# Two edits in the written order of a graph-attention and expert kernel: where layer 1 normalises its softmax, and where the plan of a layer's remainder stands

## The chip, the cores and the metric

The kernel runs on one core of a Trainium2 chip. A core has five engines that matter here: TensorE (PE) for matmuls and transposes, VectorE (DVE), ScalarE (ACT), GpSimd (POOL) and SyncE (SP), which issues most DMAs. They run side by side and wait for each other through semaphores. The metric is the device time of one execution in microseconds, as the median of several runs.

## The reference

Two layers, each of a graph attention over 128 graphs of 64 nodes and a mixture of eight experts, on 8192 rows of 256 numbers in float32:

```
x = x + elu( softmax(mask(e)) @ (LN(x) @ W) )      e[i,j] = (Wh a1)[i] + (Wh a2)[j]
                                                   layer 1: e = leaky_relu(e)
z = LN(x)
layer 0:  x = x + z + sum over the 2 best experts of w_e * (gelu(z W1_e + b1_e) W2_e + b2_e)
layer 1:  x = x +     sum over the 2 best experts of w_e * (relu(z W1_e + b1_e) W2_e + b2_e)
```

The hidden width of an expert is 256 in layer 0 and 512 in layer 1. The two weights of a row come from a softmax over its two best router scores.

## The kernel before

**Blocks.** The 8192 rows of a layer are 16 blocks of 512 rows (four tiles of 128 rows). Both layers make 32 blocks in a row. For each block a Python generator `attend` emits the attention and another, `route`, emits normalisation, router and the writing of each row into the lists of its two experts in DRAM. A `yield` ends a stage; a call `a(i)` or `r(i)` emits the next stage of block i.

**Slots.** Expert work comes in slots of 256 rows of one expert. The expert of a slot is known only on the chip: `plan` (L560 to 602) works out with small DVE instructions, every time a block has been routed, which expert lists can fill the next four slots, and writes the numbers into a table; SP reads the table into registers and fetches rows (`fetch`, L682) and weights (L733 to L741). What is left in the lists at the end is handled by `fill_up` and `rests` (L516 to 529 and L603 to 668): SP appends eight pieces of padding to the lists, DVE works out a table for 12 more slots, some of which hold two halves. That happens after block 8 and block 15 of layer 0 and after block 15 of layer 1. In this text it is "the plan of the rest".

A slot is worked in three parts: `x` (transposes px, L764, copied by DVE to xT, L768), `h` (matmuls L846, activation by ACT, L855) and `y` (matmuls L877 into py, then an addition on DVE, L884, that empties py). py has one PSUM buffer. In layer 0 the result rows go to two rows of a buffer in DRAM per token; the attention of layer 1 first adds these to its input with the weights of the router: eight DVE instructions a block, L267, "the sum of result rows". In layer 1 the weighted rows are added to the output by a DMA (L922).

**The order.** The order of instructions on PE, DVE, ACT and SP is exactly that of emission; only POOL's is left to the scheduler. The main loop (from L1038) has one step per block: t counts from 3, n = t+1. In one step the kernel finishes the attention of block n, routes block t, starts the attention of block t+2, and works four slots (five where many are waiting: `more`). The stages of `attend` that matter are, in order: the sum of result rows (L263 to 274), statistics, normalised rows, transposes, the product with W (L290), its diagonal (L301), scores and exp (L309 to L328, ending on ACT), the **normalise** (a reciprocal L334 and a product L335 on DVE), the transposes of the attention (pp, L339, and copies L341, L342), the product po (L348), and the ELU. Around the edits the loop before is:

```
        r(t)                      # router matmuls, first of the two best
        if t + 2 != NB:
            a(t + 2)              # the sum of result rows
        y()
        a(n)                      # normalise
        (h if more else x)()
        r(t)
        a(n)                      # transposes of the attention
        y()
```

Near the start of the step stands `r(t - 1)`, the last stage of the routing of the block before: `plan`, and where due `fill_up` and `rests`.

## Time and profile before

| what | us |
|---|---|
| median of 3 runs (lowest, highest) | 1437.01 (1436.83, 1442.47) |
| the profiled execution, and its span | 1675.06, 1673.3 |
| PE busy in the span | 1305.4 |
| DVE busy | 875.1 |
| POOL busy | 743.9 |
| ACT busy | 647.5 |
| mean granted clock of PE | 0.882 |

The profiled execution takes 238 us more than the runs. A line of the timeline has the start, the busy time, the engine, the line of the kernel, the operation and what it writes and reads, how many instructions are merged in it, and in brackets the idle time of that engine before it with what ended it. A line of the list of waits has the waiting instruction, the one that released it, and then the microseconds in total, how often, and the longest.

### The profile page before, as it was taken

To read this page: it belongs to the slowest core of one execution; us is meant where nothing else is said; L and a number is where in the kernel's file an instruction comes from. 1 tells how busy PE (TensorE), PEld (TensorE's weight loads), DVE (VectorE), ACT (ScalarE), POOL (GpSimd) and SP (SyncE) were. 2 spreads that over 40 slices of the span, in tenths; PEclk is the share of its full clock that TensorE was granted. 3 is DMA by queue.
4 is the path that set the end of the run, shared out by engine and by line. 5 is a ranking of instruction groups with operands and counts; after the bars stand their busy time and mean duration, and the time that the engine had idled before them with its cause. 6 is when DMAs were issued, how large, how long until landed. Compare 5 with 4: busy or idle time off the path is not lost. (4 is left out here: it accounts for less than half of the span.)

```text
span 1673.3 us, 22326 instructions
## 1 busy us (share of the span) xinstructions
PE 1305.4 (78%) x6240; PEld 1100.9 (66%) x6240; DVE 875.1 (52%) x3390; ACT 647.5 (39%) x1550; POOL 743.9 (44%) x729
## 2 busy tenths in 40 slices
PE   7657777777777667766768888988888988869994
PEld 5546665655665556555657777877777777658883
DVE  4555755574455566745565555655555654442331
ACT  5534444444433434333333434333344434223331
POOL 3164444444445543334442455444455444544324
PEclk9668988998888898788789999988889888989997
DMA  6535555575565654656765768666777656677873
GB/s 194 143 124 176 197 167 168 167 219 167 167 184 189 228 186 152 204 171 198 219 219 156 218 194 234 197 169 193 208 215 213 172 134 185 169 218 223 238 211 65
DMA packets 262829, 311.69 MB, mean 186 GB/s; under 512 B 40615, under 2 KB 219950, under 8 KB 262704
## 3 DMA queue, kind: packets, MB, share of 16 engines
q1 hardware_dynamic: 219552, 225.02, 43.7%
q0 software_dynamic: 43152, 85.24, 19.1%
q8 instruction: 50, 0.82, 0.2%
q14 instruction: 75, 0.61, 0.1%
HBM read 212.25 MB, written 99.75 MB: 186 GB/s over the span
## 5 line engine op out<-in xcount | busy, mean ns | idle before, releaser
L846 PE MATMUL ph_s<-xT_s,wc_s 128*128 128x256 f32 (+1 forms) x1760 | 402.1, 380 | 57.3 <-DVE xT_s L768 22.8
L877 PE MATMUL py_s<-wc_s,hT_s 128*128 128x256 f32 x1648 | 425.6, 411 | 21.8 <-issue 14.0
L846 PEld LDWEIGHTS ph_s<-xT_s,wc_s 128*128 128x128 f32 x1760 | 327.0, 198 | 116.3 <-DVE xT_s L768 29.9
L877 PEld LDWEIGHTS py_s<-wc_s,hT_s 128*128 128x128 f32 x1648 | 331.7, 207 | 75.9 <-issue 16.6
L922 POOL DMA_INDIRECT out_dram<-ys_s,to_s x135 | 212.8, 1576 | 366.7 <-ACT ys_s L919 215.7
L499 POOL DMA_INDIRECT lists<-tn_r,ix_r x256 | 249.5, 975 | 102.9 <-issue 71.9
L855 ACT ACTIVATE hT_s<-ph_s,wc_s 128x256 f32<-128x256 f32 (+1 forms) x440 | 175.8, 457 | 278.5 <-issue 117.2
L290 PE MATMUL pw_g<-gw,xt_g 128*128 128x258 f32 x512 | 157.6, 459 | 134.0 <-ACT wh_g L297 74.0
L893 POOL DMA_INDIRECT res<-ys_s,to_s x142 | 146.2, 1029 | 259.7 <-DVE erc_g L334 177.9
L290 PEld LDWEIGHTS pw_g<-gw,xt_g 128*128 128x128 f32 x512 | 109.5, 228 | 169.5 <-ACT wh_g L297 83.3
L768 DVE COPY xT_s<-px_s 128x512 f32<-128x512 f32 (+1 forms) x140 | 95.5, 682 | 204.4 <-remote 89.4
L884 DVE TENSOR_TENSOR ys_s<-py_s,wc_s 128x512 f32<-128x512 f32 (+1 forms) x149 | 97.4, 654 | 188.6 <-PE py_s L877 180.7
L419 PE MATMUL pl_r<-rw,xt_r 128*128 128x8 f32 x512 | 81.8, 295 | 45.4 <-DVE xt_r L255 40.9
L419 PEld LDWEIGHTS pl_r<-rw,xt_r 128*128 128x128 f32 x512 | 82.1, 246 | 51.7 <-DVE xt_r L255 45.2
L297 ACT COPY wh_g<-pw_g 128x258 f32<-128x258 f32 x128 | 47.0, 375 | 162.4 <-remote 82.0
L919 ACT ACTIVATE ys_s<-ys_s,cf_s 128x256 f32<-128x256 f32 x135 | 61.4, 500 | 105.7 <-DVE ys_s L884 105.4
L240 ACT ACTIVATE tn_r<-xb_g,nb_r,rs_r 128x256 f32<-128x256 f32 x128 | 66.5, 590 | 86.3 <-DVE nb_r L238 55.5
L240 ACT ACTIVATE xn_g<-xs,nb_g,rs_g 128x256 f32<-128x256 f32 x128 | 66.4, 590 | 66.3 <-DVE nb_g L238 66.3
L764 PE MATMUL px_s<-ident,xg_s 128*128 128x128 f32 x554 | 85.7, 278 | 0.2 <-DMA xg_s<-lists 0.2
L764 PEld LDWEIGHTS px_s<-ident,xg_s 128*128 128x128 f32 x554 | 70.7, 146 | 13.0 <-issue 1.0
L348 PE MATMUL po_g<-wh_g,pT_bd 128*128 128x256 f32 x256 | 70.8, 425 | 8.5 <-ACT pT_bd L342 7.0
L342 ACT COPY pT_bd<-pp_g 64x256 f32<-64x256 f32 x32 | 11.7, 365 | 163.7 <-DVE pT_bd L341 160.6
(503 smaller groups left out, 1583.8 us busy)
## 6 DMA issues: line engine op xcount, KB each, us to landing
wc_s<-in_w_dram SPq DMA_DIRECT2D x142, 512.0 KB
wc_s<-in_w_dram SPq DMA_DIRECT2D x156, 256.0 KB
xg_s<-lists SPq DMA_DIRECT2D x64, 260.0 KB
xg_s<-lists SPq DMA_DIRECT2D x64, 258.0 KB
yb<-res SPq DMA_DIRECT2D x16, 1024.0 KB
wc_s<-bcat SPq DMA_DIRECT2D x78, 129.0 KB
wc_s<-bcat SPq DMA_DIRECT2D x71, 130.0 KB
xs<-in_x_dram SPq DMA_DIRECT2D x16, 512.0 KB
```

The lines of the kernel that those rows point to most:

```text
L240: nc.scalar.activation(outs(t), xb[:, t, :], AF.Identity, bias=nb[:, t : t + 1], scale=rs[:, t : t + 1])
L290: nc.tensor.matmul(pw, lhsT=xt[:, k, t * P : (t + 1) * P], rhs=gw[l][:, k, :], start=(k == 0), stop=(k == KD - 1),)
L419: nc.tensor.matmul(pl[:, t, :], lhsT=tT[:, k, t * P : (t + 1) * P], rhs=rw[l][:, k, :], start=(k == 0), stop=(k == KD - 1),)
L499: ins = nc.gpsimd.indirect_dma_start(out=lists[l], out_offset=bass.IndirectOffsetOnAxis(ap=ix[:, k, t : t + 1], axis=0), in_=tn[:, t, 0 : ...
L764: nc.tensor.transpose(px[:, c, t * P : (t + 1) * P], xg[:, t, c * P : (c + 1) * P], ident)
L768: nc.vector.tensor_copy(xT[:, :, 0 : st * P], px[:, :, 0 : st * P])
L846: nc.tensor.matmul(ph[:, j, r], lhsT=w[:, o : o + P], rhs=xT[:, c, r], start=(c == 0), stop=(c == KD - 1),)
L855: nc.scalar.activation(hT[:, f + j, r], ph[:, j, r], AF.Gelu if l == 0 else AF.Relu, bias=w[:, OB1[l] + f + j : OB1[l] + f + j + 1],)
L877: nc.tensor.matmul(py[:, t, :], lhsT=hT[:, f, t * P : (t + 1) * P], rhs=w[:, O2[l] + f * D : O2[l] + (f + 1) * D], start=(f == 0), stop=(f ...
L884: nc.vector.tensor_tensor(ys[:, r, :], py[:, r, :], w[:, OB2[l] : OB1[l]].unsqueeze(1).to_broadcast([P, r.stop - r.start, D]), ALU.add,)
L893: ins = nc.gpsimd.indirect_dma_start(out=res[sl["part"]], out_offset=self.row(sl, t), in_=ys[:, t, :], in_offset=None, bounds_check=2 * N - 1,
L922: ins = nc.gpsimd.indirect_dma_start(out=out, out_offset=self.row(sl, t), in_=ys[:, t, :], in_offset=None, compute_op=ALU.add,)
```

## The change

Two things change, both in the order of emission; no instruction is added or taken away. First, the stage with the sum of result rows is cut into two stages of four instructions each. In a step whose block n belongs to layer 1 (t = 15 to 30) the order on DVE becomes: first half of the sum, normalise, second half of the sum, then `y`. In layer 0 the sum does not exist and the normalise stays behind `y`. Second, the last stage of `route` is cut in two, so that `fill_up` and `rests` come later: no longer behind `plan` near the start of the step, but in a new call `r(t - 1)` near its end, between the third or fourth `y` and the last routing stages of block t. The counts of the other calls are adapted so that every other stage stands where it stood.

```diff
-        if l > 0:
-            for t in range(TT):
+        for i in range(2):
+            for t in range(TT * l * i // 2, TT * l * (i + 1) // 2):
                 for k in range(2):
                     nc.vector.scalar_tensor_tensor(
...
-        yield
+            yield
         stats = ln_stats(xs, name)
...
         if b - (CUT if b >= CUT and l == 0 else 0) >= LAG:
             slots.take(l, b, SB, plan(l, f"p{l}_{b}", SB))
+        yield
         if b == NB - 1 or (l == 0 and b == CUT - 1):
             fill_up(l, b)
             slots.take(l, b, SF, rests(l, f"p{l}_{b}r"), True)
...
         r(t)
+        early = n < len(blks) and blks[n]["l"] == 1
+        if t + 2 != NB:
+            a(t + 2)
+        if early:
+            a(n)
         if t + 2 != NB:
             a(t + 2)
         y()
-        a(n)
+        if not early:
+            a(n)
         (h if more else x)()
         r(t)
         a(n)
         y()
-        a(t + 2, 1 + (t + 2 == NB))
+        a(t + 2, 1 + 2 * (t + 2 == NB))
...
         y()
         a(t + 2)
+        r(t - 1)
         r(t)
         r(t)
         y()
...
-    r(len(blks) - 1)
+    r(len(blks) - 1, 2)
     slots.fetch()
```

More of the change, by code (lines that the diff above doesn't have):

```diff
@@ L995, in adj_ffn_kernel @@
     load(FIRST)
-    a(0, 2)
+    a(0, 3)
     make_gw(0)
     a(0)
-    a(1, 2)
+    a(1, 3)
     token2 = counted("token2", [P, NT], [[2 * P, NT]], 0, 2)
@@ L1002, in adj_ffn_kernel @@
     place = counted("place", [P, ST], [[P, ST]], 0, 1)
-    att = lambda b: [(a, b)] * 9 + [(a, b, 2), (a, b)]
+    att = lambda b: [(a, b, 2)] + [(a, b)] * 8 + [(a, b, 2), (a, b)]
     chains = [
@@ L1008, in adj_ffn_kernel @@
         (8, att(3) + [(r, 3)] * 2),
-        (12, [(a, 4)] * 3),
+        (12, [(a, 4, 2), (a, 4), (a, 4)]),
     ]
@@ L1035, in adj_ffn_kernel @@
         turn += 1
-    r(2)
+    r(2, 2)
     slots.fetch()
```

## The prediction, made before the changed kernel was run

> **What bounds the kernel now.** I read the page first, then the list of waits, then the stretch of the timeline around the normalise of the softmax in several steps, and then the places where the plan of the rest stands and is to stand.

> ```profile
> PE 1305.4 (78%) x6240; PEld 1100.9 (66%) x6240; DVE 875.1 (52%) x3390; ACT 647.5 (39%) x1550; POOL 743.9 (44%) x729
> ...
> PE pp_g L339 <- DVE ee_g L335: 25.2, 19, 4.3
> ...
> PE pp_g L339 <- DVE l_r L445: 18.3, 5, 7.6
> ```

> TensorE (PE) is the busiest engine, so what counts is time in which PE waits. The transposes of the attention (pp, L339) wait for VectorE (DVE). 7.1 us of the first wait line lie in layer 0, and so does one wait of 7.6 in the second (its releaser was last to report; the normalise stands just ahead of it). Layer 1, which alone is changed, has 18.1 + 10.7 = **28.9 us in 16 steps**. Two such places, the second in a late step (t = 22), the first at t = 15:

> ```profile
> 641.06 3.75 DVE L267 SCALAR_TENSOR_TENSOR xs<-yb,cs,xs 128x256 f32<-128x256 f32 x8
> 641.46 0.60 PE L764 MATMUL px_s<-ident,xg_s 128*128 128x128 f32 x4
> 644.72 0.69 DVE L884 TENSOR_TENSOR ys_s<-py_s,wc_s 128x512 f32<-128x512 f32 x1
> 645.53 0.43 DVE L335 TENSOR_TENSOR ee_g<-ee_g,erc_g 128x256 f32<-128x256 f32 x1
> 646.10 1.04 PE L339 MATMUL pp_g<-ident,ee_g 128*64 128x128 f32 x4 [4.04 <-DVE ee_g L335]
> 646.93 3.62 PE L877 MATMUL py_s<-wc_s,hT_s 128*128 128x256 f32 x8
> ...
> 1046.91 3.75 DVE L267 SCALAR_TENSOR_TENSOR xs<-yb,cs,xs 128x256 f32<-128x256 f32 x8
> 1051.80 0.60 PE L764 MATMUL px_s<-ident,xg_s 128*128 128x128 f32 x4
> 1052.00 0.69 DVE L884 TENSOR_TENSOR ys_s<-py_s,wc_s 128x512 f32<-128x512 f32 x1 [1.35 <-PE py_s L877]
> 1052.82 0.42 DVE L335 TENSOR_TENSOR ee_g<-ee_g,erc_g 128x256 f32<-128x256 f32 x1
> 1053.38 0.60 PE L339 MATMUL pp_g<-ident,ee_g 128*64 128x128 f32 x4 [0.98 <-DVE ee_g L335]
> ```

> See the order on DVE: eight rows of the sum (L267), the addition that empties py (L884, "y-add"), the normalise (L335); then PE may go on. At 641 DVE itself is late: PE stood for 4.04 us behind a sum that the normalise does not need. At 1052 it is PE that comes late to y-add, since its matmuls ran at half clock; the wait is 0.98. The last line at 641 also shows the price of a long wait: eight matmuls at 3.62 us, where the y of the step at 743.07 takes 1.89 for eight.

> **The profiled execution and the runs.** It took 1675.06 us (span 1673.3), the median of the runs is 1437.01: 238 us less. The waits that end on "remote" (DVE xT_s 89.4, ACT wh_g 82.0, DVE xt_r 70.4, ACT hT_s 34.4) and the half-clock stretches behind them are my candidates for that difference. So I price each part twice: as the profile has it, and with PE at full clock and no such wait. The second is the one I take for the runs.

> [...] the waits of 4.04 and 4.26 before pp are followed by transposes of 1.04 instead of 0.60; of the two waits of 2.98, one is followed by full clock (0.60, then eight matmuls in 1.89) and one by matmuls at half. [...] So the written order counts, as the lines at 641 show. [...] Here 128x8 takes 0.17 us and 128x256 takes 0.42, which is why some forty tiny instructions of a plan add up to 8 us.

> **Part 1, the normalise between two halves of the sum (16 steps, t = 15 to 30).** No instruction is added or removed. The sum is eight instructions at 0.467 us from start to start, so each half is 1.87. The reciprocal and normalise take 0.62 from the end of y-add to the next DVE work. What is behind them now: half the sum and y-add, which end 0.62 later than before. Who waits for y-add: the next y matmuls, since py has a single PSUM buffer. **That wait takes the place of the one removed and caps the gain.**

> The normalise needs the exp sums of ACT: at 641 these end at 641.36, while the first half sum would end at 642.93. No new wait there.

> - t = 15, 16: L335 would be out at 641.06+1.87+0.62 = 643.55 and y-add at 643.55+1.87+0.69 = 646.1; y starts then instead of 646.93. Gain 0.75 (at 694, by the same sum, 0.8): 1.55.
> - t = 17 to 20, where the step has five slots: the same sum gives y at 742.56 for 743.07, 790.96 for 791.47, 843.86 for 844.75 and 896.46 for 896.96. Gain 2.3.
> - t = 21 to 29, as profiled: y-add ends at 1052.69 either way, px at 1052.40, so pp starts 0.98 earlier and y follows it. Gain 9 x 0.98 = 8.8. At full clock: counted from the end of the router's matmuls, DVE needs 0.2 + 1.5 (seven small instructions) + 3.75 + 0.6 + 0.62 = 6.7 to release pp, and PE is free after 3.62 + 0.6 = 4.2. After the change, pp runs at 4.2, but y waits for y-add until 0.2 + 1.5 + 3.75 + 0.62 + 0.69 = 6.8 instead of 6.7 + 0.5. Gain 0.4 each, 3.6.
> - t = 30 has no sum behind it: 0.98.

> Sum: 13.6 as profiled, **8.4 at full clock**.

> The clock comes on top: at t = 15 pp, y and po took 1.04 + 3.62 + 2.71 = 7.4 us, at full clock 0.60 + 1.89 + 1.89 = 4.4: 3.0 lost. Four waits (4.04, 4.26, 2.98, 2.92) were followed by such a stretch. The change breaks each into two shorter ones with pp between. Bounds: nothing, and 4 x 3.0 = 12, or more if late steps at full clock suffer it too; I take **4**, since DVE's chain to po hides part.

> **Part 2, the plan of what is left, moved (t = 9 and 16; the third plan, at the end, stays).**

> ```profile
> 676.57 0.16 DVE L519 CAST bi<-at_r 128x8 int32<-128x8 f32 x1
> ...
> 684.57 0.17 DVE L667 TENSOR_SCALAR bu_p_15r<-du_p_15r 128x8 f32<-128x8 f32 x1
> 684.65 0.42 DVE L301 TENSOR_TENSOR sm_g<-imod,wh_g 128x256 f32<-128x256 f32 x1
> 685.12 0.70 PE L309 MATMUL pe_g<-sm_g,same 128*128 128x256 f32 x2 [0.82 <-DVE sm_g L301]
> ...
> 708.63 1.97 PE L877 MATMUL py_s<-wc_s,hT_s 128*128 128x256 f32 x8 [0.47 <-issue]
> 711.72 0.68 DVE L768 COPY xT_s<-px_s 128x512 f32<-128x512 f32 x1
> 712.46 1.99 PE L846 MATMUL ph_s<-xT_s,wc_s 128*128 128x256 f32 x8 [0.55 <-issue]
> ```

> It is 8.1 us of DVE in front of L301. PE waits only 0.82 there (1.09 at t = 9), but PE had come late after waits of 6.0 and 7.5. Without these, counted from the first h of the step, PE would reach pe after about 7.9 us (h 1.9, px 0.6, then pw, h and pt_r with ACT's copies between); DVE could start xT at 2.5 and needs 0.9, 3.6 for the ordinary plan and 0.45 for L301: 7.4. Slack 0.5, so the plan costs 7.6 now (an estimate from these rows). In the new place it stands behind DVE's work of 708.51. PE has y, px and pt_g left, then h at 712.46 wants xT, which DVE delivers after the plan; DVE runs there with no gap. All 8.1 is exposed. **Difference +0.5 each**, +1 in all; bounds from -1 (if ACT or PE slips ahead of DVE) to 8.1 - 0.8 = +7.3 each, the profile's own case.

> The queues: SP issues eight list writes with it (7.7 us at 350.79), after waiting for L519. Behind them now come three weight loads, then four or five list reads that need the plan's table, and the next block's loads; before, four reads and weights. All serve work half a step or more away (weights go four slots ahead), with PE standing in the meantime. Cost nothing; if that cover is gone, h waits for weights, a few us. POOL's scatters of the next stage come 8 us later, with everything else. What comes next runs at half clock either way; after the new place it is h, px and pw, on PE's path, while before it was partly y beside the DVE sum: +2 in all.

> **Sum for the runs:** -8.4 - 4 + 1 + 2 = -9.4: 1437.0 - 9.4 = **1428**. In the profile's own prices, 1675 would see -13.6, less some clock, and +13 to +15 for the plans, about nothing.

> **Rivals.** *The cap alone* (0.33): half-clock stretches stay as they were, y waits for y-add as computed: -8.4 + 3, 1432. For it: [...] pp is a short burst of 0.5 us between two idles. *The plan is bared* (0.21, slower): at t = 9 and 16 the old place was covered in the runs as in the profile, the new one is not: 2 x 7.3, and a half-clock stretch of 3 behind each, 14.6 + 6 - 8.4 = +12, 1449. It decides from about 4 us lost per plan. For it: the 0.82 measured; against: the 238 us that runs do not have. *The clock stays up everywhere* (0.06): at full clock the late steps' waits are 2.5 us each, long enough to halve it sometimes; ten times up to 3.0 saved at most, near 1408. That the change is not carried out is excluded for DVE and PE, whose order is written; POOL's is not, and may shift by a microsecond either way.

> **Numbers.** My forecast has 0.40. About 0.5% (7.2 us) is what a measurement of this kernel can tell. Faster: 0.40 + 0.06. Same: 0.33. Slower: 0.21. The range 1414 to 1446 leaves out most of the last rival's gain and half of the slower one.

> **What would show it.** Right: pp of layer 1 without a wait for L335; instead y (L877) waits for DVE L884, about 2 us at t = 15 to 19; matmuls behind pp at full clock there. L301 at t = 9 and 16 following the ordinary plan at once, and h (L846) of the next step waiting about 8 us for xT. Wrong: pp waits still; waits for weights or lists at t = 10 and 17; or a loss of over 4 us per plan, which would turn the sign.

## The result, and the profile after

The changed kernel takes **1427.29 us** (median of 6 runs, 1425.70 to 1430.12) against 1437.02 for the kernel before (6 runs, 1436.69 to 1442.47): ratio **0.9925 [0.9906, 0.9945]**, 9.7 us less. The forecast was 1428, with "faster" the likeliest.

The profile of the kernel after was taken in an execution that agrees with the runs (span 1425.5). The first profile of before, the one the prediction read, did not. So a second one of the unchanged kernel was taken (run e0, 1440.78 us, some 3 us above the median of that kernel), and comparisons of traces below are with that one unless another is named. First the two pages, before and then after; the rows are the span, the busy times and the clock in 40 slices:

```profile
span 1439.0 us, 22326 instructions
PE 1219.4 (85%) x6240; PEld 1044.5 (73%) x6240; DVE 875.1 (61%) x3390; ACT 647.6 (45%) x1550; POOL 742.9 (52%) x729
PEclk9767999989999988999999999999999999989997
```

```profile
span 1425.5 us, 22327 instructions
PE 1212.6 (85%) x6240; PEld 1037.7 (73%) x6240; DVE 875.2 (61%) x3390; ACT 647.9 (45%) x1550; POOL 742.0 (52%) x729
PEclk9767999999999989998999999999999999999997
```

DVE does the same work in the same time. PE is busy 6.8 us less with the same 6240 matmuls: they ran at a higher clock (0.950 granted in the mean, 0.944 before). The rest of the 13.5 us between these two executions is waiting. The list of PE's waits (total, times, longest), before and then after:

```profile
PE pp_g L339 <- DVE ee_g L335: 38.2, 19, 4.0
PE ph_s L846 <- DVE xT_s L768: 37.3, 40, 3.9
PE pe_g L309 <- DVE sm_g L301: 15.7, 4, 5.6
PE pp_g L339 <- DVE l_r L445: 12.2, 5, 3.0
PE py_s L877 <- DVE ys_s L884: 8.2, 10, 1.9
```

```profile
PE ph_s L847 <- DVE xT_s L769: 49.0, 38, 7.4
PE py_s L878 <- DVE ys_s L885: 34.3, 25, 1.9
PE pp_g L339 <- DVE ee_g L335: 14.6, 20, 1.9
PE pe_g L309 <- DVE sm_g L301: 4.6, 2, 4.1
PE pp_g L339 <- DVE l_r L445: 1.4, 1, 1.4
```

(L846, L877 and L884 have become L847, L878 and L885.) The wait of pp for the normalise fell from 38.2 + 12.2 to 14.6 + 1.4. y's wait for the y-add rose from 8.2 to 34.3: most of what left one line came back in another, as the prediction's cap says. In the same way pe's wait for L301 shrank by 11.1 and h's for xT grew by 11.7: that is the plan of the rest. A late step shows the first exchange (t = 23 of before, then t = 22 of after):

```profile
870.50 0.60 PE L764 MATMUL px_s<-ident,xg_s 128*128 128x128 f32 x4
872.44 0.68 DVE L884 TENSOR_TENSOR ys_s<-py_s,wc_s 128x512 f32<-128x512 f32 x1
873.24 0.42 DVE L335 TENSOR_TENSOR ee_g<-ee_g,erc_g 128x256 f32<-128x256 f32 x1
873.81 0.60 PE L339 MATMUL pp_g<-ident,ee_g 128*64 128x128 f32 x4 [2.71 <-DVE ee_g L335]
874.24 3.62 PE L877 MATMUL py_s<-wc_s,hT_s 128*128 128x256 f32 x16
```

```profile
818.30 0.60 PE L765 MATMUL px_s<-ident,xg_s 128*128 128x128 f32 x4
818.66 0.43 DVE L335 TENSOR_TENSOR ee_g<-ee_g,erc_g 128x256 f32<-128x256 f32 x1
819.23 0.60 PE L339 MATMUL pp_g<-ident,ee_g 128*64 128x128 f32 x4 [0.33 <-DVE ee_g L335]
820.84 0.68 DVE L885 TENSOR_TENSOR ys_s<-py_s,wc_s 128x512 f32<-128x512 f32 x1
821.58 3.72 PE L878 MATMUL py_s<-wc_s,hT_s 128*128 128x256 f32 x16 [1.74 <-DVE ys_s L885]
```

One wait of 2.71 has become two, 0.33 and 1.74, with 0.60 us of transposes between. From the start of px to the start of y it is 3.74 us before and 3.28 after. Measured from one pp to the next, an undisturbed late step (one with no half clock in it) took 44.79 us before and 44.34 after (medians of five and of eight): **0.45 each, predicted 0.4**.

The other part of the gain is the clock. In the late steps (t = 21 to 29) three of the nine waits of before were followed by 3.41 us of half clock, which made the step 1.5 to 1.9 us longer (46.29 to 46.47 for 44.6 to 44.8). In the trace after the change none was; what that is worth as evidence stands in the last section. Over the whole trace PE spent 163.0 us at half clock before and 143.3 after.

### The profile page after: what moved, and what is told of

Same layout as the page of the kernel before. It is cut to its first block, busy times and chain, and to the rows that moved or that the text cites. A ratio compares the mean times of both kernels' runs of the same rounds, so it can differ in the third digit from the quotient of the medians.

```text
span 1425.5 us, 22327 instructions
## 1 busy us (share of the span) xinstructions
PE 1212.6 (85%) x6240; PEld 1037.7 (73%) x6240; DVE 875.2 (61%) x3390; ACT 647.9 (45%) x1550; POOL 742.0 (52%) x729
## 5 line engine op out<-in xcount | busy, mean ns | idle before, releaser
L847 PE MATMUL ph_s<-xT_s,wc_s 128*128 128x256 f32 (+1 forms) x1760 | 395.0, 376 | 69.3 <-DVE xT_s L769 49.0
L878 PE MATMUL py_s<-wc_s,hT_s 128*128 128x256 f32 x1648 | 393.7, 388 | 48.3 <-DVE ys_s L885 34.3
L847 PEld LDWEIGHTS ph_s<-xT_s,wc_s 128*128 128x128 f32 x1760 | 320.0, 194 | 124.9 <-DVE xT_s L769 62.5
L878 PEld LDWEIGHTS py_s<-wc_s,hT_s 128*128 128x128 f32 x1648 | 307.9, 192 | 97.2 <-DVE ys_s L885 42.3
L885 DVE TENSOR_TENSOR ys_s<-py_s,wc_s 128x512 f32<-128x512 f32 (+1 forms) x149 | 97.3, 653 | 162.4 <-PE py_s L878 158.2
L290 PE MATMUL pw_g<-gw,xt_g 128*128 128x258 f32 x512 | 124.8, 395 | 15.9 <-DVE xt_g L255 12.8
L290 PEld LDWEIGHTS pw_g<-gw,xt_g 128*128 128x128 f32 x512 | 96.5, 196 | 35.5 <-issue 13.0
L279 POOL TENSOR_SCALAR cap_g<-adj 128x256 f32<-128x256 int32 x32 | 35.1, 1096 | 81.6 <-DMA adj<-in_adj_dram 56.9
L419 PEld LDWEIGHTS pl_r<-rw,xt_r 128*128 128x128 f32 x512 | 65.4, 200 | 5.1 <-ACT xt_r L257 2.9
L342 ACT COPY pT_bd<-pp_g 64x256 f32<-64x256 f32 x32 | 11.7, 364 | 126.0 <-DVE pT_bd L341 125.9
## 6 DMA issues: line engine op xcount, KB each, us to landing
yb<-res SPq DMA_DIRECT2D x16, 1024.0 KB, 11.7
```

The source lines that it names most:

```text
L290: nc.tensor.matmul(pw, lhsT=xt[:, k, t * P : (t + 1) * P], rhs=gw[l][:, k, :], start=(k == 0), stop=(k == KD - 1),)
L847: nc.tensor.matmul(ph[:, j, r], lhsT=w[:, o : o + P], rhs=xT[:, c, r], start=(c == 0), stop=(c == KD - 1),)
L878: nc.tensor.matmul(py[:, t, :], lhsT=hT[:, f, t * P : (t + 1) * P], rhs=w[:, O2[l] + f * D : O2[l] + (f + 1) * D], start=(f == 0), stop=(f ...
L885: nc.vector.tensor_tensor(ys[:, r, :], py[:, r, :], w[:, OB2[l] : OB1[l]].unsqueeze(1).to_broadcast([P, r.stop - r.start, D]), ALU.add,)
```

## The experiments

The runs e0 to e7 are read against the kernel before at 1437 to 1438 us (e0 to e3 were timed on one chip, with 1438.06; e4 to e7 on another, with 1437.24). The last four, e8 to e11, ran on a third chip, on which the kernel before itself took 1684.56 us (38 runs, 1676.27 to 1691.47); they are read only against that. Diffs are against the changed kernel unless they say otherwise.

**e0: the kernel before, unchanged, profiled again.**

> The kernel before once more, for a profile without the 238 us between its first profile and its runs. My theory: span near 1436, no waits of 4 to 10 us on "remote"; in layer 1 pp (L339) waits about 2.5 us for the normalise in the late steps and 3 to 4 us at t = 15 to 19; pe (L309) waits about 7 us behind the plan of the rest at t = 9 and 16. Rival (the plan was covered): pe waits about 1 us there. Rival (the cap alone): as mine, but with no half-clock stretch behind the late waits, and as many elsewhere as the changed kernel has.

1440.78 us in the one run, span 1439.0, with no wait that ends on "remote". It is the "before" of the lines above.

**e1 and e2: each part alone.** e1 keeps the halved sum and the early normalise, with the plan where it stood:

```diff
         if b - (CUT if b >= CUT and l == 0 else 0) >= LAG:
             slots.take(l, b, SB, plan(l, f"p{l}_{b}", SB))
-        yield
         if b == NB - 1 or (l == 0 and b == CUT - 1):
...
-        r(t - 1)
         r(t)
         r(t)
```

e2 keeps the moved plan, with the normalise behind `y`:

```diff
-        early = n < len(blks) and blks[n]["l"] == 1
         if t + 2 != NB:
             a(t + 2)
-        if early:
-            a(n)
         if t + 2 != NB:
             a(t + 2)
         y()
-        if not early:
-            a(n)
+        a(n)
```

> Part 1 alone: the normalise between the halves of the sum, the plan of the rest in its old place. My theory: -8.4 for the cap and -4 for the clock, 1437 - 12 = 1425, so 2 to 3 us faster than the changed kernel. Rival (the gain comes from the plan): about 1437. Rival (the cap alone): 1428 to 1429.

> Part 2 alone: the plan of the rest in its new place, the normalise behind y as before. My theory: +3, 1440. Rival (the plan is bared): 1437 + 14 to 20 = 1451 to 1457. Rival (the gain comes from the plan): about 1427.

Before them 1438.06 (27 runs). e1: 1426.39, ratio 0.9911 [0.9880, 0.9943]. e2: 1438.10 (22 runs), ratio 0.9996 [0.9982, 1.0009]. So **the normalise is the whole gain, and moving the plan is worth nothing**, with an interval from 2.6 us less to 1.3 us more. The first of the two moved plans, at t = 9, shows why. First the old place (e0), then the new one (after; e2 has the same wait of 7.42); the timeline of PE:

```profile
309.25 1.22 PE L309 MATMUL pe_g<-sm_g,same 128*128 128x256 f32 x2 [5.60 <-DVE sm_g L301]
310.26 1.06 PE L310 MATMUL pe_g<-wh_g,ident 128*128 128x256 f32 x2
311.12 3.42 PE L419 MATMUL pl_r<-rw,xt_r 128*128 128x8 f32 x16
314.39 3.76 PE L877 MATMUL py_s<-wc_s,hT_s 128*128 128x256 f32 x8
```

```profile
332.20 3.57 PE L847 MATMUL ph_s<-xT_s,wc_s 128*128 128x256 f32 x8 [7.42 <-DVE xT_s L769]
335.61 0.60 PE L765 MATMUL px_s<-ident,xg_s 128*128 128x128 f32 x4
336.05 1.25 PE L290 MATMUL pw_g<-gw,xt_g 128*128 128x258 f32 x5
```

The wait is 1.82 longer in the new place. But the half clock costs less there, because it begins while PE still waits. The next two lines show the half-clock stretch at the old place (e0) and at the new one (e2): its start and end, its length, PE's busy time in it with the number of matmuls, the granted clock, and the DMA's share and GB/s:

```profile
308.65:318.89 10.24, 9.64 (x32) 0.50 0.84 206
329.75:339.99 10.24, 5.73 (x16) 0.50 1.04 254
```

Of the same 10.24 us, 9.64 slowed matmuls at the old place (pe 1.22, the router's pl 3.42, y 3.76 and px 1.06, which at full clock, in after, take 0.60, 1.85, 1.97 and 0.60) and 5.73 at the new one; in the trace after, the stretch was 6.83 with 3.23 on matmuls. The two steps together (from the pp of t = 8 to that of t = 10) took 72.23 us in e0 and 71.52 in e2.

**e3: the second half of the sum behind the second y of the step.** If y waits for the y-add behind that half, moving the half further back should free it.

```diff
         if early:
             a(n)
-        if t + 2 != NB:
-            a(t + 2)
         y()
...
-        a(t + 2, 1 + 2 * (t + 2 == NB))
+        a(t + 2, 2 + (t + 2 == NB))
```

> The changed kernel, with the second half of the sum behind the second y instead of ahead of the first y-add. It takes away what the cap rests on: y-add no longer stands behind half a sum. My theory (y waits 1.74 for y-add in each of 16 steps of the changed kernel, and that wait is on PE's path): about 1.3 us a step come back, since xT is 0.4 later: 1427 - 20 = 1407. Rival (the wait is not on the path, DVE's own chain sets the step): 1427, or slower by the delay of the statistics.

1420.40, ratio 0.9881 [0.9852, 0.9910], where 1407 was expected. Undisturbed late steps took 42.87, which is 1.47 less than after the change: the cap is y's wait for the y-add. But in the steps with five slots (t = 17 to 20) h now waited 3.1 to 3.4 us for xT, whose copy by DVE stood behind the half sum, and three of these four waits met half clock; together those four steps took 6.1 us more than after the change.

**e4: the normalise ahead of the whole sum.** pp comes as early as can be, and y still waits for the y-add behind all eight rows. If the cap alone decides, this equals the changed kernel.

```diff
         early = n < len(blks) and blks[n]["l"] == 1
-        if t + 2 != NB:
-            a(t + 2)
         if early:
             a(n)
         if t + 2 != NB:
-            a(t + 2)
+            a(t + 2, 2)
         y()
```

> The changed kernel, with the normalise ahead of the whole sum instead of between its halves. pp is let go 1.9 us earlier, y-add is not: DVE has the same work in front of it. My theory (y-add is the cap): 1427 as the changed kernel, late steps 44.3 us. Rival (what counts is when pp starts): 0.3 us a step less, about 1422. Rival (the first half of the sum was covering the exp on ACT): DVE stands for the exp sums, 1429 or more.

1434.06 (16 runs), ratio 0.9972 [0.9951, 0.9993], where the change has 0.9925: 0.0047 of 1437, or **6.8 us, are gone** (a difference of two ratios, each against its own runs of the kernel before; their intervals do not meet). That expectation fell. In the undisturbed late steps the cap held to the hundredth (44.34 in both). The rival of a wait for the exp sums is out: DVE waited 0.2 us for them, once. The loss lies at the half-clock stretches. PE at t = 17, e4 and then after:

```profile
604.76 0.60 PE L339 MATMUL pp_g<-ident,ee_g 128*64 128x128 f32 x4
608.10 3.19 PE L878 MATMUL py_s<-wc_s,hT_s 128*128 128x256 f32 x8 [2.73 <-DVE ys_s L885]
611.08 1.06 PE L765 MATMUL px_s<-ident,xg_s 128*128 128x128 f32 x4
```

```profile
605.07 0.60 PE L339 MATMUL pp_g<-ident,ee_g 128*64 128x128 f32 x4 [0.55 <-DVE ee_g L335]
607.43 1.99 PE L878 MATMUL py_s<-wc_s,hT_s 128*128 128x256 f32 x8 [1.76 <-DVE ys_s L885]
609.26 0.60 PE L765 MATMUL px_s<-ident,xg_s 128*128 128x128 f32 x4
```

With the wait in one piece (2.73) y takes 3.19 and px 1.06; with 2.31 in two pieces (0.55 and 1.76) they take 1.99 and 0.60. From the pp of t = 17 on, e4 had four more stretches of 3.41 us at half clock in its steps up to t = 29 (at t = 17, 18, 19 and 21), and these four steps were 1.4 to 2.4 us longer than after the change, 6.9 in all.

**e5: the plan further back, behind `x`, and e7: e5 and e6 together.** In the two steps concerned (`due = t in (CUT, NB)`):

```diff
-        r(t - 1)
         r(t)
-        r(t)
+        due = t in (CUT, NB)
+        if not due:
+            r(t)
         y()
...
+        if due:
+            r(t - 1)
+            slots.fetch()
+            r(t)
```

> The changed kernel, with the plan of the rest (and, in these two steps, the stage that works out the places in the lists) behind the last y and x of the step, so that xT of that x is made before it. The changed kernel's h waits 7.4 us for xT at t = 9 and 16. My theory (that wait is the bare length of the plan): h and the next px go on beside it, 2.5 us of cover each, 1427 - 5 = 1422. Rival (what is won at h is lost at the next product with W, since ACT and the routing come later): 1427.

> e5_plan_behind_x and e6_half_later_where_four together. My theory: the two act at different steps and add up, 1427 - 5 - 13 = 1409. Rival (the plan's place brings nothing): as e6_half_later_where_four, 1414.

e5: 1434.33 (22 runs), ratio 0.9970 [0.9954, 0.9985], slower than the change. The wait did not go, it only moved to the next consumer. PE in e5 at t = 9:

```profile
335.22 1.23 PE L290 MATMUL pw_g<-gw,xt_g 128*128 128x258 f32 x2 [7.63 <-DVE xt_g L255]
337.12 6.03 PE L290 MATMUL pw_g<-gw,xt_g 128*128 128x258 f32 x14 [0.68 <-ACT xt_g L257]
```

It is 7.63 instead of 7.42, since the stage that places rows in the lists (2.2 us of DVE here) stands ahead of xt_g as well, and the half clock lasts 10.2 us instead of 6.8, mostly over pw. e7: 1417.57, ratio 0.9857 [0.9826, 0.9888]; it loses 4.1 us to e6, so that e5's part costs there too. The late steps of e5 have the order of the changed kernel; one of them, at t = 21, ran into half clock all the same (46.00 us).

**e6: as e3, but only in steps with four slots**, where no x stands between:

```diff
         if early:
             a(n)
-        if t + 2 != NB:
+        late = early and not more and t + 2 != NB
+        if t + 2 != NB and not late:
             a(t + 2)
...
-        a(t + 2, 1 + 2 * (t + 2 == NB))
+        a(t + 2, 1 + 2 * (t + 2 == NB) + late)
```

> As e3_half_later, but only in steps with four slots; those with five (t = 17 to 20) keep the order of the changed kernel. In e3_half_later the late steps fell from 44.35 to 42.87 us, and the steps with five slots grew, with 3.1 to 3.4 us of h waiting for xT. My theory: 9 x 1.47 = 13 from the late steps, t = 17 to 20 as in the changed kernel: 1414. Rival (the loss was the clock's chance, not the order): 1420 as e3_half_later.

**1413.43** (6 runs, 1408.20 to 1413.88), ratio **0.9821 [0.9789, 0.9853]**: the best version, 13.9 us below the change. The steps t = 20 to 29 together took 435.3 us instead of 448.6, which is 13.3 of it. A late step of e6, PE:

```profile
818.16 0.60 PE L765 MATMUL px_s<-ident,xg_s 128*128 128x128 f32 x4
819.01 0.60 PE L339 MATMUL pp_g<-ident,ee_g 128*64 128x128 f32 x4 [0.25 <-DVE ee_g L335]
819.52 3.72 PE L878 MATMUL py_s<-wc_s,hT_s 128*128 128x256 f32 x16
```

Beside the last fence on after's late step: the 1.74 ahead of y is gone.

**e10: the kernel before, with PE kept busy while it waits.** Ahead of pp, in the steps of layer 1, 14 more transposes of the identity go into a PSUM tile that nothing reads. The wait for the normalise stays where it is. Against the kernel before:

```diff
+    def warm(name, n):
+        pd = ps_c.tile([P, TB], F32, tag="r", name=f"warm_{name}")
+        for i in range(n):
+            nc.tensor.transpose(pd[:, i % 4 * P : (i % 4 + 1) * P], ident, ident)
...
         r(t)
+        if NB <= n < len(blks):
+            warm(f"{t}", 14)
         a(n)
```

> The kernel before with 14 such transposes ahead of pp in the 16 steps of layer 1, where PE waits 1.8 to 4 us for the normalise. It parts the two terms of my sum: the wait stays, only the clock behind it can change. Theory (the clock is a term of its own, about half of the gain): 1437 - 5 to 7 = 1430 to 1432. Rival (the cap alone made the gain): 1437.

1681.48 (14 runs) against 1684.56: ratio 0.9975 [0.9957, 0.9993], about 4.2 us of 1684.56 less, bounds 1.2 and 7.2; 5 to 7 was expected. Nothing in it lets pp start earlier, so this is the clock by itself. In its trace the steps t = 15 to 20 took 302.4 us with 57.9 at half clock; in the first profile of before, which shows the same "remote" waits, 306.4 with 84.4. The late steps gained nothing there: 51.2 us each in both.

**e8, e9 and e11: three more combinations, inconclusive.** e8 is e6 with the plan in its old place. e9 is e4 with `warm(12)` behind pp. e11 is e6 with `warm(54)` ahead of the first h of the steps t = 10 and 17, which waits behind the moved plan.

> e6_half_later_where_four with the plan of the rest back in its old place. My theory (the two places cost the same: a wait of 5.6 us with a half-clock stretch over the router and y, or one of 7.4 with a stretch over h): 1413 to 1415. Rival (the new place is worth something once the rest is faster): 1417 or more. Rival (it costs what I had priced, 3): 1410.

> e4_normalise_first with 12 transposes of the identity, read by nobody, behind pp in the 16 steps: PE does something in the wait of 2.2 to 3.6 us for y-add. No data and no wait is changed. Theory of the clock (e4 loses to the changed kernel only because its one long wait is followed by half clock more often): 1427 or a little less. Rival (something else in that order costs the 7 us): 1434, or more by what the transposes take.

> e6_half_later_where_four with 54 such transposes at t = 10 and 17, in the 7.4 us in which h waits for xT behind the plan of the rest. The half-clock stretch behind that wait was 6.8 to 10.2 us long. Theory of the clock: 2 x 2 to 3 us less, 1413 - 5 = 1408. Rival (DVE and ACT set the pace there and hide the half clock): 1413.

e8: 1676.53, ratio 0.9958 [0.9941, 0.9975]. e9: 1682.53 (22 runs), ratio 0.9988 [0.9974, 1.0001]. e11: 1679.99 (9 runs), ratio 0.9967 [0.9953, 0.9982]. On this chip even the step that helps most elsewhere is worth 0.4%, and neither e6 nor e4 ran there, so whether the plan's old place or the extra transposes improve on them stays open.

## Why the prediction was right

**The cap held.** "That wait takes the place of the one removed and caps the gain": y's wait for the y-add grew by 26.1 us in the list, e3 and e6 removed it from the late steps and gained 1.5 us a step, and e4, which brings pp earlier still, gained nothing in them. The sizes: 0.4 predicted for a late step, 0.45 measured. At t = 15, from the time PE is free to the start of y: 4.25 + 0.60 - 0.16 = 4.69 in e2 (the old order; y starts 0.16 before pp's modelled end) and 1.63 + 0.60 + 1.74 = 3.97 after, so 0.72 for the predicted 0.75. At t = 17 it is 0.51 for 0.51. Counted so over all 16 steps it is 9.3 us (e2 against after) and 8.2 (e0 against e1), for 8.4. What the prediction drew from a profile that was 238 us too long was right because it counted from the end of the router's matmuls with full-clock durations, not from the waits shown.

**The clock was put in the wrong place.** The term was 4, an estimate of the author's, for "four waits (4.04, 4.26, 2.98, 2.92)" in the steps t = 15 to 20; late steps that "suffer it too" stood only in the bound. At t = 15 to 20 the gain is not shown. From the y behind pp of t = 14 to that of t = 20, half clock fell from 34.1 us (e0) to 23.9 (e1) with the plan in its old place, but rose from 23.9 (e2) to 30.7 (after) with the plan in its new one. "Matmuls behind pp at full clock there" was a sign named for being right, and at t = 15 and 16, and behind the first y of t = 18, it did not come. PE at t = 15, after:

```profile
526.84 0.60 PE L339 MATMUL pp_g<-ident,ee_g 128*64 128x128 f32 x4 [1.63 <-DVE ee_g L335]
529.18 3.03 PE L878 MATMUL py_s<-wc_s,hT_s 128*128 128x256 f32 x8 [1.74 <-DVE ys_s L885]
```

Nor did pp run "without a wait for L335": 7.5 us of it are left in layer 1. The late steps do suffer: the late waits of before are 2.54 to 2.73 us, not the 0.98 of the first profile, and three of nine were followed by half clock in e0 and three of nine in e2. By these traces that is three times some 1.7 us, 5.1, in the late steps alone. That the size came near 4 is luck. The stretches at half clock measure 3.41, 6.83, 10.24 us and so on; the last section has what PE did ahead of them. The rival *cap alone* spoke of pp as "a short burst" that would not keep the clock up. e4 against the change speaks the other way: the 0.60 us of transposes in the middle of the wait instead of ahead of it went with 6.8 us. e10, on the third chip, adds its 4.2. The medians by themselves would not exclude the rival: with the plan at zero its 8.4 us lie within the interval of the change (7.9 to 13.5 us); the half-clock stretches of the traces and e10 speak against it. The rival *the clock stays up everywhere* held in the late steps of after and e1 alone: 30.7 us of half clock remain at t = 15 to 20 after the change.

The total was met all the same: e1's 11.7 us (1438.06 - 1426.39) stand against 8.4 + 4 = 12.4, and the change's 9.7 against 9.4. The last agreement is in part luck too: the plan's +3 did not come, and part 1 brought somewhat less than 12.4.

**The plan came to zero, not +3.** Both prices were too high and too close: "the plan costs 7.6 now" was 5.60 at t = 9 and 5.54 at t = 16; "all 8.1 is exposed" was 7.42 and 7.43. The 8.1 had gaps in it; here the plan took 6.9 us of DVE, from 321.39 to 328.26. So the new place waits 1.85 longer (7.425 - 5.57), where +0.5 was put. The next step, +2 for half clock "on PE's path", had the wrong sign at t = 9: of stretches of the same 10.24 us, 9.64 fell on matmuls at the old place and 5.73 at the new one. The two about cancelled; e2's interval, -2.6 to +1.3 us, leaves out the +3. The rival *the plan is bared* needed 4 us a plan and is excluded by e2. Of the transfers behind it, neither list reads nor weights brought a new wait of PE's.

(The prediction's second place, at 1052, is t = 23 and not 22; no sum rests on it.)

**The 238 us.** The candidates, waits on "remote" and the half clock behind them, fit: e0's list of waits has no line with "remote" (a wait for which the profile shows no instruction that ended it). What went unsaid is that this is no matter of a profile. On the third chip plain runs took 1684.56, and the waits there read like the first profile; the list of DVE's waits in e10:

```profile
DVE xT_s L768 <- remote: 110.3, 13, 11.5
DVE xt_r L255 <- remote: 72.6, 11, 7.0
```

What makes these waits was not tried.

## What to carry to other kernels

When a wait is taken away, look for the next user of what the late engine still owes, here a PSUM tile that one addition must empty, and count to that; then move that debt too, as e6 did, but only where nothing on the path stands behind it. Count waits of PE twice, once for their length and once for the half clock behind them, which came here behind three of nine late waits of 2.54 to 2.73 us (e0) and made the step 1.5 to 1.9 us longer. Work that must be done anyway, put into the middle of a wait, can save some of the second (6.8 us between e4 and the change), but not in every step: at t = 21 the same two waits of 0.27 and 1.74 were followed by full clock in after and by half clock in e5. Price steps from an execution that takes as long as the runs do; where there is none, count with the undisturbed durations from one common starting point, and don't add up the waits shown.

## What the runs showed of the hardware that was not expected

```profile
779.69:783.10 3.41, 0.68 (x7) 1.00 0.74 213
783.10:786.52 3.42, 3.42 (x10) 0.50 0.97 299
775.74:779.16 3.42, 1.99 (x9) 1.00 0.58 104
779.16:782.57 3.41, 3.41 (x18) 1.00 0.93 337
779.56:782.97 3.41, 1.39 (x10) 1.00 0.67 207
782.97:786.38 3.41, 3.41 (x10) 0.50 0.78 231
```

PE was busy 20%, 58% and 41% of these windows. So waits of 2.54 to 2.73 us were followed by half clock in six of 18 late steps (e0 and e2), when one window held enough of the wait (busy 20 to 38%); the one of 2.12 to 2.21 in e4 in one of nine (36%); the divided ones in none of 18 (after and e1), but in one of nine in e5. None of 18 is weaker than it looks: a step of 44.34 us is 12.99 windows, so that the nine late steps of one trace meet the grid at nearly the same place and are little more than one case.

And the same kernel took 1437 us on some chips and 1684 on another, with waits on DVE and ACT that end on "remote" in the second case (up to 11.5 and 7.0 us in e10, which ran there).
